# A Perceiver block on one core: keys first, vectors worked out three batches behind their loads, the last output product in another round

## Chip, core and metric

The kernel runs on one core of a Trainium2 chip. The metric is the device time of one execution in microseconds (us). The time before is the median of three runs.

The core has five engines that run side by side, each working through its own instructions in order: TensorE (PE; its weight loads are shown apart as PEld) multiplies matrices, VectorE (DVE), ScalarE (ACT) and GpSimd (POOL) work on vectors, and SyncE (SP) issues the DMAs here. [...] On-chip data lie in SBUF; matmul results lie in PSUM.

## What is computed

Cut to what matters:

```python
x   = x + ln(softmax(q k^T) v @ w_out)      # cross attention: q from layernorm(x), k and v from
                                            # the context (512 rows) and from the latents (64 rows)
x   = x + Wo(rms(softmax(..) - lambda * softmax(..)) @ v)   # differential self attention with rotary q, k
x   = x + down(fp4(silu(gate(fp4(x))) * up(fp4(x))))        # feed-forward, weights fp4 too
```

There are 16 batches, each of 64 latents by 512 (eight tiles of 128 rows, two batches to a tile) and a context of 512 by 512. Cross attention has 8 heads of 64. Self attention takes lambda from four vectors of 32 values (`lambda_q1` and so on), and it scales and shifts its normed output by `ln_w` and `ln_b`, 64 values each. The feed-forward has 1408 hidden columns; its inputs and weights are rounded block by block to fp4.

## The kernel before

Matrices are split into a high and a low half (a rounded copy, and the difference), and each product is the sum of three: high by high, high by low, low by high. `Common.product` (L109) issues them one after the other: for 512 rows of contraction these are 12 matmuls. The high half is usually a ScalarE cast, the low half a subtraction on VectorE or GpSimd in turn.

**Latents** (L427). Tiles 0 and 1 of x are loaded and normed first; `turn` (L478) transposes a tile on TensorE, scales and shifts it with ScalarE (L489) and makes its halves on VectorE (L491, L492). Then, for four groups of two tiles, `heads` (L553) projects q and k (four products of 12 matmuls each), and `values` (L582) projects v (two products). Results go to DRAM scratch and are read back by the batches later. `during(n, ...)` (L541) hangs other work behind the n-th product: splitting weights, the context's weights, the first contexts. In group 0 q comes first, and its evictions lag by two products, because they add `cw.bq`, which `bias` (L494) and `bias_sum` (L505) work out. All weight pieces pass through nine buffers of the tag `raw`.

**Cross attention** (L670). The loop over 16 batches (L927) is an order written out by hand: `keys` and `values` (TensorE, four products each), `scores`, `softmax`, the transposes `turn` and `turn_both`, `finish` for the batch before, and pieces of the next context (`cx.high`, `cx.low`, `cx.stats`, `cx.fetch`). Ten times in a batch it calls `quant.tick()`, which moves the feed-forward's weights along: 35 pieces, a new one every fourth tick, each of ten steps (L260, L163) over all three vector engines and SP. In odd batches from 3 on a finished tile p passes through `out_turn`, `out_product` and `out_norm`, and one batch later through `out_moments`. In batch 2 `att.sa.load()` (L396) loads the vectors of self attention and at once works out lambda. `load_o` and `weight_o` bring `w_out` in batch 0.

**From cross to self attention** (L1021 to L1040) the last tile's output, the splitting of self attention's weights and tile 0 of self attention are interleaved by hand. Then `rest` (L1285) takes a tile n a round: products Wq, Wk and Wv, `rope` (rotations: VectorE, and a last sum on GpSimd, L1122), `end` (L1264: transposes, scores, softmax and sums of tile n, weighing of tile n-1), while tiles n-1 and n-2 are mixed, scaled, turned and projected out.

Up to the end of `rest`, `in_order` (L82) pins each engine's instructions to the order of the program; past it a planner orders the feed-forward by itself. Products share three PSUM buffers of the tag `mm` (transposes too), two pairs of the tag `sim`, and one of the tag `av`.

## Time and profile before

| what | us |
|---|---|
| median of 3 runs (lowest, highest) | 960.89 (959.71, 962.38) |
| the profiled execution | 962.64 |
| its span, first to last instruction | 960.9 |
| its mean granted TensorE clock | 0.984 |

The stages, by windows of the trace: busy us of TensorE, VectorE, ScalarE and GpSimd, and the clock granted to TensorE.

| stage | from, to | PE | DVE | ACT | POOL | clock |
|---|---|---|---|---|---|---|
| first loads and norms | 0, 12 | 2.51 | 5.14 | 6.25 | 4.60 | 1.00 |
| latents, group 0 up to the values | 12, 38 | 24.01 | 16.18 | 11.28 | 8.93 | 0.87 |
| latents, groups 1 to 3 | 38, 88 | 50.00 | 25.58 | 29.22 | 20.59 | 1.00 |
| batch 0 | 93.3, 124.2 | 27.41 | 14.81 | 11.67 | 9.49 | 1.00 |
| batches 1 and 2 | 124.2, 183.3 | 58.03 | 47.09 | 29.88 | 22.85 | 1.00 |
| batch 3, to its output product | 183.3, 214.3 | 26.89 | 21.22 | 11.45 | 9.85 | 0.89 |
| one pair of batches later on | 276.9, 338.1 | 61.19 | 48.64 | 28.68 | 25.86 | 1.00 |
| cross to self attention | 595.6, 634.5 | 32.93 | 23.18 | 13.21 | 20.88 | 0.91 |
| self attention, rounds 3 to 7 | 650, 740 | 83.04 | 70.33 | 31.27 | 42.08 | 1.00 |
| feed-forward | 740, 961 | 208.84 | 169.10 | 57.01 | 26.77 | 0.98 |

How to read it: where TensorE's busy time falls short of a stage's length, it waited; where the clock is under 1.00, its matmuls in part of that stage ran slower than elsewhere. A row of the timeline gives start, length, engine and line, what is written and read, the count, and in brackets the idle time of the engine before it with what ended that. Idle time of another engine costs only if TensorE comes to wait for it.

### The profile page before, as it was taken

The numbers are of one execution on the slowest core, as the hardware profiler recorded it, in microseconds if no ns is written. First come the engines' busy times: TensorE is split into PE (matmuls) and PEld (weight loads), VectorE is DVE, ScalarE is ACT, GpSimd is POOL, SyncE is SP. The second block draws the span as 40 slices with busy tenths as digits, with TensorE's granted clock in tenths as the row PEclk, the third lists the DMA queues.
The fourth block names the chain that finished last, engine by engine and source line by source line (L and its number), as shares of the span: only waits on it lengthen the run. The fifth ranks groups of instructions, "written<-read, shape, count | busy, mean of one in ns | idle before, by whom it ended". The sixth has DMA issues, their size and how long they took to land.

```text
span 960.9 us, 17488 instructions
## 1 busy us (share of the span) xinstructions
PE 911.9 (95%) x6773; PEld 751.3 (78%) x6773; DVE 684.4 (71%) x1396; ACT 383.7 (40%) x738; POOL 332.3 (35%) x362
## 2 busy tenths in 40 slices
PE   5999899999999999999999999889997899999998
PEld 4998677778877878778787888678776688888886
DVE  6434577677788777887787733757878677888875
ACT  4464254443444444444444335333333222222221
POOL 4155253235435353252542504543544320100000
PEclk9999999989999999999999999989999899999999
DMA  6564655544545445454553242400008230000000
GB/s 218 177 230 143 177 183 163 141 136 137 176 140 161 145 144 160 124 161 140 181 171 111 71 124 67 181 18 2 1 1 336 92 121 1 23 12 12 12 12 22
DMA packets 80546, 111.12 MB, mean 116 GB/s; under 512 B 33472, under 2 KB 39120, under 8 KB 79184
## 3 DMA queue, kind: packets, MB, share of 16 engines
q1 hardware_dynamic: 80304, 109.48, 35.4%
q8 instruction: 53, 0.87, 0.4%
q0 software_dynamic: 160, 0.52, 0.2%
q14 instruction: 29, 0.24, 0.1%
HBM read 84.26 MB, written 25.72 MB: 114 GB/s over the span
## 4 chain that ended last, share of the span: by engine, by line
PE 70%; DVE 14%; ACT 5%; issue 4%; DMA 3%; POOL 2%; SPq 1%; ACTq 0%; DVEq 0%; POOLq 0%
PE pk L116 14%; PE pv L116 14%; PE gu L116 10%; PE dn L116 6%; PE av L845 3%; PE sim L777 3%; PE po L116 3%; PE lk L116 2%; PE lq L116 2%; PE lv L116 2%; PE prt L154 2%; PE Wv L116 1%; DVE x L351 1%; DMA dT<-d_d 1%; PE Wq L116 1%
## 5 line engine op out<-in xcount | busy, mean ns | idle before, releaser
L116 PE MATMUL pk<-x,xkh 128*128 128x512 f32 x512 | 132.0, 400 | 2.1 <-DVE k L751 2.1
L116 PE MATMUL pv<-xvh,x 128*128 128x512 f32 x512 | 133.4, 392 | 0.6 <-ACT prT L812 0.6
L116 PEld LDWEIGHTS pk<-x,xkh 128*128 128x128 f32 x512 | 94.8, 190 | 28.0 <-issue 4.4
L116 PEld LDWEIGHTS pv<-xvh,x 128*128 128x128 f32 x512 | 95.2, 188 | 24.2 <-ACT prT L812 4.1
L751 DVE TENSOR_TENSOR k<-pk,row 128x512 f32<-128x512 f32 x64 | 43.9, 686 | 51.9 <-PE pk L116 51.5
L116 PE MATMUL gu<-gT,fx 128*128 128x512 f32 (+1 forms) x288 | 68.7, 387 | 2.8 <-ACT fx L123 2.8
L116 PE MATMUL pk<-x,xkl 128*128 128x512 f32 x256 | 69.4, 393 | 0.0
L116 PE MATMUL gu<-uT,fx 128*128 128x512 f32 (+1 forms) x288 | 68.8, 384 | 0.0
L116 PE MATMUL pv<-xvl,x 128*128 128x512 f32 x256 | 68.5, 389 | 0.0
L800 ACT ACTIVATE pr<-pr,least 128x576 f32<-128x576 f32 x64 | 49.2, 772 | 42.1 <-DVE least L796 41.0
L351 POOL TENSOR_TENSOR x<-raw,x 128x512 fp32r<-128x512 f32 x32 | 44.8, 1401 | 60.3 <-ACT x L345 60.3
L764 ACT ACTIVATE v<-pv,rs 128x512 f32<-128x512 f32 x64 | 43.7, 685 | 53.1 <-PE pv L116 53.0
L116 PEld LDWEIGHTS gu<-gT,fx 128*128 128x128 f32 x288 | 54.3, 194 | 11.5 <-ACT fx L123 3.1
L116 PEld LDWEIGHTS gu<-uT,fx 128*128 128x128 f32 x288 | 52.9, 192 | 7.5
L116 PEld LDWEIGHTS pk<-x,xkl 128*128 128x128 f32 x256 | 48.6, 190 | 10.5
L116 PEld LDWEIGHTS pv<-xvl,x 128*128 128x128 f32 x256 | 48.0, 188 | 10.2
L796 DVE CUSTOM_DVE_ANT_0 pr<-sim,mask 128x576 f32<-128x576 f32 x64 | 45.5, 748 | 7.4 <-PE sim L777 6.9
L116 PE MATMUL dn<-dT,hh 128*128 128x512 f32 x176 | 44.9, 394 | 0.6 <-ACT hh L123 0.6
L304 DVE BATCH_NORM_STATS2 cst<-nat 128x6 f32<-128x512 f32 x64 | 42.9, 670 | 0.0
L845 PEld LDWEIGHTS av<-v,prT 128*64 128x64 f32 x1024 | 36.8, 138 | 5.9 <-issue 5.9
L845 PE MATMUL av<-v,prT 128*64 128x64 f32 x1024 | 41.1, 224 | 0.0
L777 PE MATMUL sim<-k,mask 64*64 64x288 f32 x512 | 39.5, 415 | 0.4 <-DMA mask<-q_d 0.4
(298 smaller groups left out, 1952.6 us busy)
## 6 DMA issues: line engine op xcount, KB each, us to landing
nat<-in_ctx_dram SPq DMA_DIRECT2D x16, 1024.0 KB
raw<-in_ctxT_dram SPq DMA_DIRECT2D x64, 256.0 KB
d_d<-qhl_d SPq DMA_DIRECT2D x11, 512.0 KB
row<-rs_d SPq DMA_DIRECT2D x16, 256.0 KB
g_d<-qhl_g SPq DMA_DIRECT2D x8, 512.0 KB
u_d<-qhl_u SPq DMA_DIRECT2D x8, 512.0 KB
gT<-g_d SPq DMA_DIRECT2D x4, 1024.0 KB
uT<-u_d SPq DMA_DIRECT2D x4, 1024.0 KB
```

Source lines behind the costliest of these rows:

```text
L116: self.nc.tensor.matmul(ps, lhsT=p[i], rhs=p[j], start=start and n == 0, stop=stop and n == last)
L154: self.nc.tensor.transpose(pt[:, c * P : (c + 1) * P], src[:, c * P : (c + 1) * P], self.ident)
L304: nc.vector.bn_stats(st, self.nat[b][:, j, :])
L351: by.tensor_tensor(lo, self.raw[:, c, :], f32(hi), ALU.subtract)
L751: nc.vector.tensor_tensor(k[:, S : S + N], ps, cx.row[b], ALU.mult)
L764: nc.scalar.mul(v, ps, cx.rs[b][:, t : t + 1])
L777: nc.tensor.matmul(pss[r][c * S : (c + 1) * S, h, :half], lhsT=queries[b % 2][rows, m, :], rhs=st["k"][m][rows, at : at + half], start=Tru ...
L796: nc.vector.tensor_tensor_reduce(two(pr), ps[:, :, :half], two(mask), -1.0, BIG, ALU.add, ALU.min, least)
L800: nc.scalar.activation(pr, pr, AF.Exp, bias=least, scale=-1.0, accum_out=st["tot"][:, t : t + 1])
L845: nc.tensor.matmul(st["av"][rows, 2 * a + r, :], lhsT=w[:, rows], rhs=v[:, at : at + S], start=(n == 0), stop=(n == len(pairs) - 1),)
```

## The change

It has seven parts.

1. *Latents.* k's weights are loaded and split ahead of q's, and each group projects k before q. In group 0 the first three k products run their two high-weight sums first (`terms`, `late`), and the low-weight sums follow. Tile 1 is scaled and shifted by VectorE and not by ScalarE, and the halves are made in a call of their own, `halves`. The bias sums of q come behind k's products.
2. *Vectors of self attention.* `sa.load()` in batch 2 only issues the six DMAs of cos, sin and lambda's vectors; `sa.work()` in batch 5 does the arithmetic. `ln_w` and `ln_b` are loaded as rows at the start, transposed by TensorE behind the 17th product, and scaled out of PSUM.
3. *Quantiser.* In batch 0 seven of the ten ticks are left out.
4. *out_turn.* The four ScalarE casts are issued first, then the four VectorE subtractions.
5. *out_norm* is cut in two: the three GpSimd operations are now `out_add`.
6. *Cross to self attention.* Rotations follow their products directly, `sum(0)` is moved past `split("Wo", 0, 1)`, tile 1's products move into this part, the last `out_product` comes behind tile 1's products, `out_norm` behind `end(1)`.
7. *rest* starts at n = 2; there the last tile's `out_add` and `out_moments` come after `out(0)`.

```diff
+    def terms(self, ps, parts, ks, start=True, stop=True):
         terms = [(0, 2), (0, 3), (1, 2)]
...
                 n += 1
+            yield
...
-        lv = cm.const.tile([P, 4, HEAD_DIM], F32, tag="lv", name="lv")
+        self.lv = cm.const.tile([P, 4, HEAD_DIM], F32, tag="lv", name="lv")
         for n, name in enumerate(("lq1", "lq2", "lk1", "lk2")):
-            nc.sync.dma_start(lv[:, n, :], i[name].partition_broadcast(P))
+            nc.sync.dma_start(self.lv[:, n, :], i[name].partition_broadcast(P))
+
+    def work(self):
+        cm, nc, lv = self.cm, self.cm.nc, self.lv
         nc.vector.tensor_tensor(lv[:, :2, :], lv[:, :2, :], lv[:, 2:, :], ALU.mult)
...
-        with nc.allow_non_contiguous_dma(reason="a vector onto partitions"):
-            for n, name in enumerate(("ln_w", "ln_b")):
-                for h in range(2):
-                    nc.sync.dma_start(
-                        self.lnwb[h * S : (h + 1) * S, n : n + 1],
-                        i[name].rearrange("(p o) -> p o", o=1),
-                    )
-        nc.vector.tensor_scalar_mul(self.lnwb, self.lnwb, 1.0 - LAMBDA_INIT)
+    def load_norm(self, pool):
+        self.rows = pool.tile([2, P], F32, tag="lnwb", name="lnwb_rows")
+        for n, name in enumerate(("ln_w", "ln_b")):
+            for h in range(2):
+                self.cm.nc.sync.dma_start(
+                    self.rows[n : n + 1, h * S : (h + 1) * S],
+                    self.i[name].rearrange("(o p) -> o p", o=1),
+                )
+
+    def turn_norm(self):
+        cm, nc = self.cm, self.cm.nc
+        pt = cm.ps_av.tile([P, D], F32, tag="av", name="lnwb_t")[:, :2]
+        nc.tensor.transpose(pt, self.rows, cm.ident[:2, :2])
+        nc.vector.tensor_scalar(self.lnwb, pt, 1.0 - LAMBDA_INIT, None, ALU.mult)
...
-            nc.scalar.activation(ln[:, k, :], src, AF.Identity, bias=bias, scale=scale)
+            if p == 1:
+                nc.vector.tensor_scalar(ln[:, k, :], src, scale, bias, ALU.mult, ALU.add)
+            else:
+                nc.scalar.activation(ln[:, k, :], src, AF.Identity, bias=bias, scale=scale)
+        rows[p] = ln
+
+    def halves(p):
+        g, n = divmod(p, GT)
+        ln = rows.pop(p)
...
-        lag = 2 if (g, what) == (0, "q") else 0
+        late = 3 if (g, what) == (0, "k") else 0
...
+            made.append((m, ps, terms))
+            if m < late:
+                next(terms)
+                next(terms)
+            if m < late - 1:
+                continue
+            for at, done, steps in made:
+                for _ in steps:
+                    pass
+                then()
+                take(at, done)
+            made = []
...
+    weight("k", *range(KC))
     weight("q", *range(KC))
-    weight("k", *range(KC))
...
-    split("q", w_q, 0)
+    high("k", w_k, 0)
     turn(0)
-    split("q", w_q, 1)
     turn(1)
-    split("q", w_q, 2, 3)
+    halves(0)
+    for k in range(1, KC):
+        high("k", w_k, k)
+    halves(1)
     for k in range(KC):
-        high("k", w_k, k)
+        low("k", w_k, k)
     for k in range(KC):
-        bias("q", k)
+        high("q", w_q, k)
+    for k in range(KC):
+        low("q", w_q, k)
...
+    sa.load_norm(pool)
     cx.load(0)
-    during(1, bias_sum, "q", cw.bq, S**-0.5)
     for k in range(KC):
-        during(k // 2, low, "k", w_k, k)
+        during(0, bias, "q", k)
+    during(3, bias_sum, "q", cw.bq, S**-0.5)
+    during(16, sa.turn_norm)
...
+        heads(g, "k", w_k, sc.k, 1.0)
         heads(g, "q", w_q, sc.q, S**-0.5, cw.bq)
-        heads(g, "k", w_k, sc.k, 1.0)
...
             nc.scalar.activation(oh[:, k, :], src, AF.Identity, bias=bias)
+        for k in range(KC):
+            src, bias = pt[:, k * P : (k + 1) * P], cw.bv[:, k : k + 1]
             nc.vector.scalar_tensor_tensor(
...
+        state["oz", p] = z
+
+    def out_add(p):
+        z = state.pop(("oz", p))
         nc.gpsimd.tensor_tensor(z, z, rows_o["g_o"], ALU.mult)
...
+        def tick():
+            if b:
+                quant.tick()
...
-        quant.tick()
+        tick()
...
             out_norm(done)
+            out_add(done)
...
+        if b == 5:
+            att.sa.work()
...
-    out_moments(NT - 2)
     att.product(0, "Wq")
     att.split("Wv", 0, 1)
     finish(B - 1)
+    att.rope(0, "Wq")
     att.split("Wv", 2, 3)
     att.norm(1)
     att.product(0, "Wk")
+    att.rope(0, "Wk")
     out_turn(NT - 1)
-    att.rope(0, "Wq")
     att.product(0, "Wv")
-    att.rope(0, "Wk")
+    att.values(0)
+    out_moments(NT - 2)
+    att.end(0, sum=False)
+    att.split("Wo", 0, 1)
+    att.sum(0)
+    att.product(1, "Wq")
+    att.mix(0)
+    att.product(1, "Wk")
+    att.rope(1, "Wq")
+    att.product(1, "Wv")
+    att.values(1)
+    att.rope(1, "Wk")
+    att.norm(2)
     out_product(NT - 1)
-    att.values(0)
-    att.split("Wo", 0, 1)
+    att.split("Wo", 2, 3)
+    att.end(1)
     out_norm(NT - 1)
-    att.end(0)
-    att.split("Wo", 2, 3)
-    out_moments(NT - 1)
     assert not quant.active and not quant.jobs
+    return {2: lambda: out_add(NT - 1), 3: lambda: out_moments(NT - 1)}
...
-        for n in range(1, NT):
+        for n in range(2, NT):
...
             if n == 2:
+                last[2]()
+                last[3]()
                 ff.weights(("g", 0), ("u", 0))
             self.end(n)
```

More of the change, by code (lines that the diff above doesn't have):

```diff
@@ L107, in two, with product @@
         return self.ps_sim.tile([P, 2, D], F32, tag="sim", name=name)
-    def product(self, ps, parts, ks, start=True, stop=True):
+    def product(self, *args, **kwargs):
+        for _ in self.terms(*args, **kwargs):
+            pass
+    def terms(self, ps, parts, ks, start=True, stop=True):
         terms = [(0, 2), (0, 3), (1, 2)]
@@ L409, in load, with latents, _latents @@
         nc.vector.tensor_scalar(self.neglam, self.neglam, -LAMBDA_INIT, None, ALU.add)
-        with nc.allow_non_contiguous_dma(reason="a vector onto partitions"):
-            for n, name in enumerate(("ln_w", "ln_b")):
-                for h in range(2):
-                    nc.sync.dma_start(
-                        self.lnwb[h * S : (h + 1) * S, n : n + 1],
-                        i[name].rearrange("(p o) -> p o", o=1),
-                    )
-        nc.vector.tensor_scalar_mul(self.lnwb, self.lnwb, 1.0 - LAMBDA_INIT)
-def latents(tc, cm, sc, i, cw, cx):
+    def load_norm(self, pool):
[11 more added lines that the diff above has]
+        nc.vector.tensor_scalar(self.lnwb, pt, 1.0 - LAMBDA_INIT, None, ALU.mult)
+def latents(tc, cm, sc, i, cw, cx, sa):
     with ExitStack() as ctx:
-        _latents(ctx, tc, cm, sc, i, cw, cx)
-def _latents(ctx, tc, cm, sc, i, cw, cx):
+        _latents(ctx, tc, cm, sc, i, cw, cx, sa)
+def _latents(ctx, tc, cm, sc, i, cw, cx, sa):
     nc = tc.nc
@@ L438, in _latents @@
     source = {"q": i["w_q"], "k": i["w_kv"][:, :D], "v": i["w_kv"][:, D:]}
-    raws, lns, zs, mvs, sums = {}, {}, {}, {}, {}
+    raws, lns, rows, zs, mvs, sums = {}, {}, {}, {}, {}, {}
     def load(*tiles):
@@ L570, in heads @@
             ps = cm.mm(f"l{what}_{g}_{m}")[:, : GT * P]
-            cm.product(
-                ps, lambda k: (w[0][:, k, cols], w[1][:, k, cols], hi[:, k, :], lo[:, k, :]), range(KC)
-            )
-            made.append((m, ps))
-            then()
-            if m >= lag:
-                take(*made.pop(0))
-        while made:
-            take(*made.pop(0))
+            terms = cm.terms(
+                ps,
+                lambda k, cols=cols: (w[0][:, k, cols], w[1][:, k, cols], hi[:, k, :], lo[:, k, :]),
+                range(KC),
+            )
+            made.append((m, ps, terms))
[6 more added lines that the diff above has]
+                for _ in steps:
+                    pass
+                then()
+                take(at, done)
+            made = []
         nc.sync.dma_start(dst[g], st)
@@ L665, in _latents @@
                 turn(p)
+                halves(p)
         values(g)
@@ L878, in out_turn @@
             nc.scalar.activation(oh[:, k, :], src, AF.Identity, bias=bias)
+        for k in range(KC):
+            src, bias = pt[:, k * P : (k + 1) * P], cw.bv[:, k : k + 1]
             nc.vector.scalar_tensor_tensor(
@@ L940, in cross_attention @@
         cx.high(b + 1, 1)
-        quant.tick()
+        tick()
         if b:
@@ L951, in cross_attention @@
         cx.high(b + 1, 2)
-        quant.tick()
+        tick()
         if last:
@@ L956, in cross_attention @@
             finish(b - 1)
-        quant.tick()
+        tick()
         if last:
@@ L966, in cross_attention @@
         cx.high(b + 1, 3)
-        quant.tick()
+        tick()
         values(b, 0)
@@ L971, in cross_attention @@
         cx.stats(b + 2, 0)
-        quant.tick()
+        tick()
         if last:
@@ L982, in cross_attention @@
         cx.stats(b + 2, 1)
-        quant.tick()
+        tick()
         if b == 0:
@@ L1262, in out, with end @@
         self.nc.vector.tensor_tensor(cm.x[t], ps, cm.x[t], ALU.add)
-    def end(self, n):
+    def end(self, n, sum=True):
         if n < NT:
@@ L1281, in end, with rest @@
             self.rms(n - 1)
-        if n < NT:
+        if n < NT and sum:
             self.sum(n)
-    def rest(self, ff):
+    def rest(self, ff, last):
         norms = iter([step for t in range(2) for step in ff.norm_steps(t)])
@@ L1293, in step @@
             next(steps, lambda: None)()
-        for n in range(1, NT):
+        for n in range(2, NT):
             self.product(n, "Wq")
-            if 0 <= n - 2:
-                self.scale(n - 2)
+            self.scale(n - 2)
             self.product(n, "Wk")
             self.mix(n - 1)
-            if 0 <= n - 2:
-                self.turn_o(n - 2)
+            self.turn_o(n - 2)
             self.rope(n, "Wq")
@@ L1310, in rest @@
                 step(norms)
-            if 0 <= n - 2:
-                self.out(n - 2)
+            self.out(n - 2)
             if n >= 4:
@@ L1506 @@
     quant = Quantise(cm, sc, i)
-    latents(tc, cm, sc, i, cw, cx)
+    latents(tc, cm, sc, i, cw, cx, sa)
     w2 = ctx.enter_context(tc.tile_pool(name="work_2", bufs=1, reuse_waits="tile"))
@@ L1511 @@
     att = SelfAttention(cm, i, sa, w1, w2)
-    cross_attention(tc, cm, sc, i, cw, cx, w1, w2, att, quant)
-    att.rest(ff)
+    last = cross_attention(tc, cm, sc, i, cw, cx, w1, w2, att, quant)
+    att.rest(ff, last)
     ff.rest()
```

## The prediction

> **What bounds the kernel.** I read the page's busy shares first, then who waited for whom, asked of TensorE, then the timeline where those waits lie.

> ```profile
> span 960.9 us, 17488 instructions
> ...
> PE 911.9 (95%) x6773; PEld 751.3 (78%) x6773; DVE 684.4 (71%) x1396; ACT 383.7 (40%) x738; POOL 332.3 (35%) x362
> ...
> PE   5999899999999999999999999889997899999998
> ...
> PEclk9999999989999999999999999989999899999999
> ```

> TensorE is busy in 911.9 of 960.9 us, so only 49 us of idle time, and matmuls run at a lowered clock, can be won: no operation of TensorE leaves the program. The lower digits sit at the start, in slices 8 to 9 (168 to 216 us), and from slice 26 on.

> ```profile
> PE ot L154 <- DVE on L1234: 7.4, 4, 3.3
> ...
> PE qt L154 <- POOL rc_q L1122: 4.0, 1, 4.0
> PE po L116 <- ACT v L764: 3.2, 3, 1.1
> ...
> PE bq L509 <- DVE ws_bq L501: 2.0, 1, 2.0
> PE pk L116 <- DVE k L751: 2.1, 1, 2.1
> ...
> PE ot L154 <- DVE k L751: 2.0, 1, 2.0
> ```

> Columns: total us, times, longest. The diff touches the qt, bq and pk waits and the second ot; between 196 and 580 us TensorE has 380.2 busy of 384.

> **Part 1, the vectors' load at b = 2.**

> ```profile
> 187.97 0.23 DVE L404 TENSOR_TENSOR lv<-lv 128x64 f32<-128x64 f32 x1 [5.91 <-DMA lv<-in_lk_dram]
> 192.04 0.66 PE L154 MATMUL ot<-ident,o 128*128 128x128 f32 x4 [2.04 <-DVE k L751]
> 194.76 3.78 PE L116 MATMUL pk<-x,xkh 128*128 128x512 f32 x8 [2.07 <-DVE k L751]
> ```

> VectorE stands 5.91 us at L404 before a load that was just issued; behind it are queued the context's statistics, the quantiser and two key evictions (L751), which hold PSUM buffers, so TensorE stops twice and then runs slowly: eight matmuls in 3.78 us, against 1.98 for the same form at 186.02. From keys(3,0) at 183.30 to the output product at 214.35 is 31.05 us; the same stretch two batches on, 251.56 to 276.91, is 25.35. The whole stall is 5.7 us. Afterwards six DMAs are still issued there (2.75 us of the SP queue by the rows at 182.01 to 184.81; the lnwb four, 2.4 us, go to the start), but nothing waits for them until b = 5. There the arithmetic costs VectorE 0.23 + 0.22 + 0.16 + 0.15 and a trip through ScalarE, shown as 0.27 idle: about 1.1 us. Behind it are queued statistics, and in batch 5 VectorE idles 1.4 us or more before a key eviction (row at 254.48), so I take 0.3 lost: **-5.4**, between -6 and -4. The four lnwb row loads, one transpose and one PSUM read in the latents' second group cost under 0.3 us, beside 60 us in which TensorE never waits.

> **Part 2, the start.** Before, q's projection stops at 17.08 for the bias sums (2.0 idle), runs the sums (1.5), and restarts at half pace until 26. With k first the sums have 48 matmuls of cover. If rows held at their lone durations: first matmul at 12.1 (transpose done 9.0; four scalings on VectorE at 0.3 us, estimated from L879's 0.35 on the same 128x128 out of PSUM; halves 0.43 + 0.69 + 0.43), k's 48 matmuls by 19.4 (18 at 0.21 us, as at 11.98, the rest at 0.12), sums 1.0, q 5.8, transposes 0.9: values begin at 27.1 instead of 32.5, -5.4. But:

> ```profile
> 7.73 0.68 DVE L455 TENSOR_TENSOR wql<-raw_q,wqh 128x512 fp32r<-128x512 f32 x1
> ...
> 12.57 1.78 DVE L455 TENSOR_TENSOR wql<-raw_q,wqh 128x512 fp32r<-128x512 f32 x1
> ```

> The same instruction takes 0.68 alone and 1.78 beside a GpSimd subtraction. [...] This speaks against the change: GpSimd now has four low halves (k1, k3, q1, q3) ready from 9.9 us on, while VectorE is kept at the scalings until 10.4 and only then makes the latents' halves. Taken in turns, GpSimd holding some 1.15 us each time (the 1.78 less 0.68 gives 1.1), the halves end at 11.6, 13.4, 14.9 and 16.7, the bias at 22.4; the first matmul is at 15.0, values at 30.7. [...] I take **-1.8**; between +1 (one turn more) and -5.4.

> **Part 3, no quantiser at most of batch 0.**

> ```profile
> 110.15 0.69 DVE L177 TENSOR_REDUCE qm_g<-qw_g 128x32 f32<-128x512 f32 x1 [6.11 <-DMA qw_g<-in_w_gate_dram]
> ...
> 121.17 1.20 PE L116 MATMUL pv<-xvh,x 128*128 128x512 f32 x4 [0.57 <-ACT prT L812]
> ```

> VectorE waits 6.11 us for a weight piece, queued late behind key loads on SP; the softmax stands behind it, and TensorE idles 0.93 and 1.54 us at the transposes. Both go. But the last wait stays and grows: values(0,3) needs a PSUM buffer that the prT copy frees, and that copy is behind woh's casts, which wait for raw_wo, issued at 113.78 by an SP queue that is full from 94 on. Two removed issues bring it forward 1.2 us, and 256 KB fewer in flight about 0.9 (at 270 GB/s): **-2.2** instead of the 3.1 of idle; between -5 (batch 1's later wait of 1.07 goes too) and -0.5. Since seven ticks vanish, every later quantiser step falls on another place of its batch. The 1.0 to 1.1 us wait before the output product in four of six pairs of batches (62.6 against 61.2 us) comes from a cast (L271) ahead of v's eviction; in odd batches that cast now comes a slot earlier, but a ScalarE step that waits for VectorE (L188) takes its slot. I take **-1**: between -4.4 (four waits gone) and +3.

> Splitting out_turn's loops takes away the 0.42 us turns of ScalarE and VectorE (27.4 us of VectorE idle over eight calls), but TensorE waits there only 0.5 us, in the last call, so it is counted in part 4 alone.

> **Part 4, from cross to self attention.**

> ```profile
> 626.36 0.66 PE L154 MATMUL qt<-ident,rc_q 128*128 128x128 f32 x4 [4.05 <-POOL rc_q L1122]
> 627.76 1.12 PE L154 MATMUL kt<-ident,rc_k 128*128 128x128 f32 x4 [0.75 <-POOL rc_k L1122]
> ```

> From Wq of tile 0 (595.59) to Wq of tile 2 (634.46) is 38.9 us. The chain of waits runs out_turn, product, moments, zl, softmax, sums, out_moments on VectorE; only then come tile 1's rotations, and after 4.05 us idle the next matmuls run slowly (wt 1.97, later 1.15). Worked through again in the new order with the rows' durations: tile 0's rotations follow their products directly [...], qt 608.5, scores 610.3, Wq of tile 1 611.1 (was 613.85), softmax ends 614.3, sum and mix 619.6, tile 1's rotations on GpSimd 622.4 and 623.8; meanwhile TensorE has tile 1's products and the moved output product until 622.2. Then qt, kt, wt, zt, scores, weighing: Wq of tile 2 at 628.2, **-6.3**. Given back: out_norm's 0.8 on VectorE comes between the sums and scale, where

> ```profile
> 655.64 0.68 DVE L1234 TENSOR_TENSOR on<-o,rstd_o 128x512 f32<-128x512 f32 x1
> ...
> 656.38 0.65 PE L154 MATMUL ot<-ident,on 128*128 128x128 f32 x4
> ```

> shows no slack: ot starts as scale's result lands. With the tighter start of that round 1.4 us. And in round 2 three GpSimd products (L896 to L898, 1.3 each = 3.9) run before out_moments, where VectorE waits in order, with the next zl, softmax, sums and scale behind it: zl moves about 1.9, so +1.9 at the next ot. Part 4: **-3.0**, between -7.5 and -0.5. From round 3 on the order is the old one.

> **Sum.** -5.4 - 1.8 - 2.2 - 1 - 3.0 = -13.4. The profiled execution took 962.64 us (span 960.9 plus 1.74 around it): 949.2. It lay 1.75 above the median 960.89, so the forecast is **947.5**. The feed-forward's order beyond the fixed part is chosen by a planner and may shift by 1.5 either way.

> **Rivals.** (a) *Everything hidden is won*: VectorE and GpSimd don't take turns at the start (-5.4), the four waits vanish (-4.4), out_add's wait hides (part 4 -5): with -5.4 and -3 that is -23, about 938. For it: most stalls are single events; against: 1.78 beside 0.68. (b) *The transition and the start are given back*: GpSimd's pieces delay the first matmul, the waits at ot repeat (0 and -0.5), leaving parts 1 and 3: -5.9 - 2.2 = -8, about 953. For it: the zero slack at ot. (c) *The quantiser's new place* makes a new ScalarE wait before v's eviction, in every batch from 2 to 14. It has to eat 13.4 plus 2.9 us over 13 batches, 1.25 us each, to end slower; at 1.5 us it gives 967. For it: the present wait is 1.1 us in four odd batches. Against: even batches show none, and 384-wide pieces lost it with 0.15 us less on each row. (d) *No effect*: the removed stalls are all refilled; against it, the b = 2 stall has no work beside it.

> **Chances.** Forecast, within some 5 us: 66%; (a) 16%; (b) 12%; (c) 3%; (d) 3%. A measurement here tells about 0.3% (2.9 us) from nothing: faster 94%, same 3%, slower 3%. Range 938 to 955: it takes in (a) and (b).

> **What would show it.** Right: no VectorE idle of several us in b = 2; first lk matmul near 15 and values near 31; no L177 in batch 0 before the first softmax, and a wait of some 1.5 us at values(0,3); qt of tile 1 without 4 us of idle; a wait of 1 to 2 us at ot of tiles 0 and 1. Wrong: the first lk matmul near 12 (turns not taken) or beyond 16; waits "po <- ACT v" in most batches (c); Wq of tile 2 less than 3 us nearer to Wq of tile 0.

## The result, and the profile after

The changed kernel takes 943.75 us (943.18 to 944.45), the kernel before 960.30 (958.79 to 962.38) in the same series: ratio 0.9826, 95% interval 0.9805 to 0.9848, or 16.55 us less. In a later series it took 945.93 beside 961.20 (ratio 0.9841, 0.9828 to 0.9855), at a mean granted clock of 0.991 to 0.993 instead of 0.994 to 0.996. The forecast was 947.5, with a range of 938 to 955.

The page of the changed kernel, its first lines and the slices (span 960.9 before):

```profile
span 941.4 us, 17506 instructions
...
PE 902.7 (96%) x6774; PEld 744.8 (79%) x6774; DVE 689.1 (73%) x1400; ACT 381.9 (41%) x734; POOL 324.9 (35%) x362
...
PE   4999999999999999999999999999998799999998
...
PEclk9999999999999999999999999999999899999999
```

TensorE has one matmul more (the transposed norm rows). Of the 19.5 us between the two spans 10.3 are idle time of TensorE (49.0 before, 38.7 after) and 9.2 are busy time (911.9 before, 902.7 after). The second part is pace: the clock records of the two traces show 30.7 us at half clock before and 10.2 after, and half of that difference is 10.2. So the stops that went had cost twice, 10.3 us as idle time and 9.2 us as slow work. The lower digits of TensorE in slices 5, 26 and 27, and of the clock in slices 9 and 27, are gone. Whom TensorE waited for (total us, times, longest):

```profile
PE ot L160 <- DVE on L1300: 10.2, 6, 3.5
PE lk L121 <- DVE lnh L516: 5.7, 1, 5.7
...
PE pv L121 <- ACT prT L854: 2.3, 1, 2.3
```

The waits of before at qt (4.0 us), at bq (2.0), at pk and the second ot (2.1 and 2.0), and the three at po (3.2) are no longer in the view. The one at pv, in batch 0, has grown (0.6 before), and so have that of the first product at the start (3.0 at lq before, 5.7 at lk now, because the halves come later) and those at ot (7.4 before). Cut into stages at TensorE's first rows of each product, the two traces give (us):

| stage | before | after | difference | forecast |
|---|---|---|---|---|
| start to the first values | 32.52 | 30.65 | -1.87 | -1.8 |
| values to the first keys | 60.83 | 61.16 | +0.33 | under +0.3 |
| batch 0 | 30.68 | 31.15 | +0.47 | -2.2 |
| batch 1 | 30.29 | 28.99 | -1.30 | in batch 0's |
| batch 2 | 28.98 | 28.98 | 0 | 0 |
| batch 3 to its output product | 30.98 | 24.07 | -6.91 | -5.4 |
| on to batch 15's output product | 371.51 | 367.79 | -3.72 | -1 |
| on to Wq of tile 0 | 9.80 | 9.81 | +0.01 | 0 |
| Wq of tile 0 to Wq of tile 2 | 38.87 | 31.61 | -7.26 | -6.3 |
| Wq of tile 2 to tile 4 | 32.58 | 35.37 | +2.79 | +3.3 |
| Wq of tile 4 to the end | 289.10 | 287.14 | -1.96 | 0 |

The sum is -19.4, the spans' difference but for 0.1 us; the end here is the start of the last row of matmuls. The last row of the table is no effect of the change. Between its first gate product and that end the feed-forward took 214.37 us before and 212.71 after; in the second trace of the same changed kernel it took 215.45, and in eleven other kernels of this study, none of which touches it, 213.89 to 215.65. The windows of its first 20 us (length, busy us of PE, PEld, DVE, ACT and POOL, granted clock, DMA share, GB/s), first trace, then second:

```profile
724.00:744.00 20.00, 18.31 (x131) 15.03 (x132) 14.41 (x29) 5.56 (x8) 7.18 (x12) 0.91 0.48 168
```

```profile
723.00:743.00 20.00, 18.32 (x119) 14.84 (x120) 12.84 (x24) 5.56 (x8) 5.25 (x5) 0.77 0.48 168
```

One program, two executions, and a clock of 0.91 or 0.77 in the same 20 us. In all fourteen traces the feed-forward's length, less TensorE's idle time in it (6.4 to 8.0 us) and half of its time at half clock (6.8 to 13.0 us), is 202.5 to 203.0 us: the spread is made by these two alone. So times are compared below by their ratios, and single effects by the stage in which they lie.

### The profile page after: what moved, and what is told of

Read it like the earlier page. It is cut to its first block, busy times and chain, and to the rows that moved or that the text cites. A ratio compares the mean times of both kernels' runs of the same rounds, so it can differ in the third digit from the quotient of the medians.

```text
span 941.4 us, 17506 instructions
## 1 busy us (share of the span) xinstructions
PE 902.7 (96%) x6774; PEld 744.8 (79%) x6774; DVE 689.1 (73%) x1400; ACT 381.9 (41%) x734; POOL 324.9 (35%) x362
## 4 chain that ended last, share of the span: by engine, by line
PE 79%; DVE 11%; POOL 4%; ACT 3%; DMA 2%; issue 1%; SPq 1%; ACTq 0%; DVEq 0%; POOLq 0%
PE pv L121 18%; PE pk L121 18%; PE gu L121 10%; PE dn L121 6%; PE av L887 4%; PE sim L819 4%; PE prt L160 3%; PE lk L121 3%; PE lq L121 2%; PE lv L121 2%; PE po L121 2%; DVE ex L1228 1%; DVE mx L1227 1%; POOL rc_q L1188 1%; PE ht L160 1%
## 5 line engine op out<-in xcount | busy, mean ns | idle before, releaser
L121 PEld LDWEIGHTS pk<-x,xkh 128*128 128x128 f32 x512 | 93.7, 188 | 25.4 <-issue 3.9
L121 PE MATMUL gu<-gT,fx 128*128 128x512 f32 (+1 forms) x288 | 66.8, 379 | 2.8 <-ACT fx L129 2.8
L121 PEld LDWEIGHTS pv<-xvl,x 128*128 128x128 f32 x256 | 48.6, 190 | 10.4
L121 PEld LDWEIGHTS pk<-x,xkl 128*128 128x128 f32 x256 | 48.1, 188 | 10.3
L854 ACT COPY prT<-prt 128x512 f32<-128x512 f32 x64 | 34.1, 585 | 18.1 <-PE prt L160 18.1
```

The costliest lines, as they stand in the source:

```text
L121: self.nc.tensor.matmul(ps, lhsT=p[i], rhs=p[j], start=start and n == 0, stop=stop and n == last)
L854: nc.scalar.copy(prT, pt.rearrange("p (j q) -> p j q", q=P))
```

## The experiments

Kernels of one series ran on one chip, beside the kernel before. Times are medians.

### One stop at a time

**The vectors alone.** The kernel before, with the arithmetic at b = 5 and all else as it was:

```diff
         if b == 2:
             att.sa.load()
+        if b == 5:
+            att.sa.work()
```

> The kernel before with the vectors' arithmetic (and only it) moved from their loads at b = 2 to b = 5; the four norm rows are still loaded at b = 2, one element to a partition. The stall as costed in the prediction: VectorE's 5.91 us idle at b = 2 goes, TensorE's two waits of 2.0 and 2.1 us and the slow matmuls after them too; from the first key product of batch 3 to the output product of tile 0 the stretch falls from 31.05 to 25.4 us, and the time by 5.4 us, to about 955.4 where before is 960.84. Rival: the wait only moves to b = 5, where the norm rows' own landing or the trip through ScalarE stops VectorE in the same way: the stretch of batch 6 grows by 3 us or more, and 2 us at most are won.

956.89 beside 961.33: ratio 0.9950 (0.9935 to 0.9965), -4.4 us. Batch 3's stretch is 26.03, that is -4.95 where some 5.6 were expected: ahead of its output product TensorE now stands 1.04 us for v's eviction, a wait that the stall had covered. From batch 5's output product to batch 7's, where the arithmetic now falls, it takes 61.66, against 61.23 before: 0.4 lost, not 3. In the changed kernel the late arithmetic reads, on VectorE:

```profile
273.71 0.22 DVE L413 TENSOR_TENSOR lv<-lv 128x64 f32<-128x64 f32 x1
273.96 0.22 DVE L415 TENSOR_REDUCE dots<-lv 128x2 f32<-128x64 f32 x1
274.45 0.72 DVE L417 TENSOR_TENSOR neglam<-dots 128x1 f32<-128x1 f32 x1 [0.27 <-ACT dots L416]
```

No idle time before L413 (5.91 us before), and 0.27 for the trip through ScalarE.

**The loops of out_turn alone.** The kernel before, with one line added:

```diff
             nc.scalar.activation(oh[:, k, :], src, AF.Identity, bias=bias)
+        for k in range(KC):
+            src, bias = pt[:, k * P : (k + 1) * P], cw.bv[:, k : k + 1]
             nc.vector.scalar_tensor_tensor(
```

> The kernel before with only the loop in out_turn split in two (ScalarE's four reads of the transposed outputs first, then VectorE's four). The prediction gave this nothing in the batches. If the four waits of 1.05 us before the output product need both the quantiser's old place and the turns that ScalarE and VectorE take in out_turn (0.42 us idle each): they fall to about 0.2 us, from the output product of batch 3's round to the last one in the batches it is 369.4 instead of 371.4, and the time is 2 to 3.5 us less (with batch 3's own wait, and 0.4 before the last tile's product), about 958. If the prediction was right that the loops are worth nothing in the batches: the four waits stay at 1.05 us and the time stays within 0.5 us.

957.54 beside 961.33: ratio 0.9959 (0.9946 to 0.9973), -3.8 us for a reordering of eight instructions. From batch 3's output product to batch 15's it is 368.84 instead of 371.51, and batch 3's stretch is 0.6 shorter. The forecast had given this nothing in the batches. VectorE, ScalarE and TensorE in batch 5 before, then the same three with the loops split:

```profile
262.38 0.35 DVE L879 SCALAR_TENSOR_TENSOR ol<-ot,bv,oh 128x128 fp32r<-128x128 f32 x1 [2.25 <-ACT oh L878]
263.17 0.35 DVE L879 SCALAR_TENSOR_TENSOR ol<-ot,bv,oh 128x128 fp32r<-128x128 f32 x1 [0.43 <-ACT oh L878]
...
265.01 0.68 DVE L751 TENSOR_TENSOR k<-pk,row 128x512 f32<-128x512 f32 x1
...
274.88 0.69 DVE L270 STREAM_TRANSPOSE qhl_u<-qw_u 128x512 f32<-128x512 f32 x1
...
275.65 0.62 ACT L271 CAST qhl_u<-qhl_u 128x512 fp32r<-128x512 f32 x1 [2.88 <-issue]
276.18 0.68 ACT L764 ACTIVATE v<-pv,rs 128x512 f32<-128x512 f32 x1
...
276.91 1.20 PE L116 MATMUL po<-woh,oh 128*128 128x512 f32 x4 [1.05 <-ACT v L764]
```

```profile
263.64 1.13 DVE L881 SCALAR_TENSOR_TENSOR ol<-ot,bv,oh 128x128 fp32r<-128x128 f32 x4 [3.02 <-ACT oh L878]
264.69 0.68 DVE L751 TENSOR_TENSOR k<-pk,row 128x512 f32<-128x512 f32 x1
...
274.56 0.69 DVE L270 STREAM_TRANSPOSE qhl_u<-qw_u 128x512 f32<-128x512 f32 x1
...
275.34 0.62 ACT L271 CAST qhl_u<-qhl_u 128x512 fp32r<-128x512 f32 x1 [2.89 <-issue]
275.86 0.68 ACT L764 ACTIVATE v<-pv,rs 128x512 f32<-128x512 f32 x1
...
276.60 1.19 PE L116 MATMUL po<-woh,oh 128*128 128x512 f32 x4 [0.25 <-ACT v L764]
```

The instruction ahead of these on VectorE, L270 at 259.44 before, runs 0.48 later with the loops split, and the key eviction behind them (L751) 0.32 earlier: 0.80 gained. From that eviction to the transposition L270 (274.88 before, 274.56 with the loops split) VectorE shows no idle time in either trace, so the 0.80 arrives there whole. ScalarE's cast of its result (L271) stands ahead of v's eviction, and TensorE's wait falls from 1.05 to 0.25: the same 0.80, some twenty VectorE instructions and twelve microseconds further on.

**The quantiser's place**, from both sides: the changed kernel with the old place, and the kernel before with the new one.

```diff
-        self.clock, self.active = 0, []
+        self.clock, self.active = 3, []      # in the changed kernel
+        self.clock, self.active = 1, []      # in the kernel before
```

> The changed kernel with the quantiser's counter started at 3 instead of 0, so that from batch 1 on every step of the quantiser falls on the same place of its batch as before the change, while batch 0 stays free of it. If the four waits of some 1.05 us before the output product (TensorE for v's eviction on ScalarE) are made by the place of the quantiser's steps alone: the four come back, the stretch from the first key product of batch 1 to the last output product of the batches is 4 to 5 us longer, and the time rises by 4 to 5 us to about 948.5. If instead the relief of batch 0 or the vectors' move took those waits away: none comes back and the time stays within 1 us of 943.7.

> The kernel before with the quantiser's counter started at 1 instead of 0, nothing else: the steps fall where the changed kernel has them, batch 0 keeps its quantiser. Place alone: the four waits of 1.05 us vanish, 4 to 5 us less than before, about 956 where before is 960.3; in batch 0 VectorE's wait for the weight piece may move by one step, within 1 us. If the place is worth what the prediction took, it is 1 us less; if a new ScalarE wait comes in its place (the prediction's third rival), it is slower.

The first took 947.19 beside 960.84 (ratio 0.9853, 0.9831 to 0.9874); its four executions spread over 5.5 us, and by the ratios it is 0.1 to 0.3% longer than the changed kernel, within the intervals. By stages: batch 3 is 24.54 (24.07), and on to batch 15's product 369.45 (367.79), so 2.1 us, not 4 to 5; the waits come back as 0.2 us. The second took 961.91 beside 960.84 (ratio 1.0004, 0.9996 to 1.0013): nothing. It wins 1.86 us on the way to batch 15, and loses 2.07 in batch 3, where VectorE's idle time before the vectors' load is 7.55 us instead of 5.91:

```profile
189.45 0.22 DVE L404 TENSOR_TENSOR lv<-lv 128x64 f32<-128x64 f32 x1 [7.55 <-DMA lv<-in_lk_dram]
```

In the rest of its trace batch 0 is 1.62 shorter and batch 1 2.14 longer than before. Together with the loops, in the stretch from batch 3's to batch 15's output product (us):

| | old place | new place |
|---|---|---|
| loops joined | 371.51 | 369.65 |
| loops split | 368.84 (alone), 369.45 (with the other edits) | 367.79 |

The two figures of the changed kernel (369.45 and 367.79) contain the arithmetic of the vectors, too, 0.4 us in the run with the vectors alone. Either edit alone takes most of the 1.05 us waits (0.25 with the loops, 0.08 to 0.25 with the place); of the stretch the loops take the larger part.

**The output weight's loads ahead of batch 0**, in the changed kernel:

```diff
     around(1, 0, 1)
+    load_o(0)
+    load_o(1)
     for b in range(B):
...
-        if b == 0:
-            load_o(0)
-            load_o(1)
         values(b, 1)
```

> The changed kernel with the loads of the output weight's first two row blocks issued ahead of batch 0 instead of in its middle. If TensorE's 2.31 us before the fourth value product of batch 0 comes from woh's casts waiting for those loads, and the slow matmuls after it (1.89 us for four, 1.07 elsewhere) from that wait: both go, batch 0 from its first key product to that of batch 1 falls from 31.15 to about 27.2, and the time falls by about 4 us to 939.7. If the slow matmuls have another cause: 2.3 us less, and the row of 1.9 us stays. If the load only takes the place of another one on the same queue (the keys' ends or the queries of batch 0): the wait reappears at the scores of batch 0 and the time falls by less than 1 us.

941.62 beside 960.84: ratio 0.9795 (0.9779 to 0.9811). Batch 0 is 27.21; TensorE no longer waits at pv, the matmuls there keep their pace (1.98 us for eight), and at the scores it waits 0.85 us for the queries (0.6 in the changed kernel), so the wait did not move there. ScalarE and TensorE of the changed kernel, first trace, then TensorE of its second:

```profile
116.50 0.62 ACT L129 CAST woh<-raw_wo 128x512 fp32r<-128x512 f32 x1 [4.48 <-DMA raw_wo<-in_w_out_dram]
...
117.89 1.07 ACT L854 COPY prT<-prt 128x512 f32<-128x512 f32 x2
```

```profile
118.52 1.89 PE L121 MATMUL pv<-xvh,x 128*128 128x512 f32 x4 [2.31 <-ACT prT L854]
120.21 1.91 PE L121 MATMUL pv<-xvl,x 128*128 128x512 f32 x4
121.91 1.21 PE L121 MATMUL pv<-xvh,x 128*128 128x512 f32 x4
```

```profile
118.08 1.20 PE L121 MATMUL pv<-xvh,x 128*128 128x512 f32 x4 [2.24 <-ACT prT L854]
119.12 1.08 PE L121 MATMUL pv<-xvl,x 128*128 128x512 f32 x4
```

The cast waits 4.48 us for raw_wo, the prT copy stands behind it, the values behind the copy, as forecast. After 2.31 us the matmuls run at nearly half their pace for some 3.4 us (the three rows begin 3.39 us apart, first to last, against 1.96), which costs about 1.5 more; after 2.24 us in the second execution they don't (its third row begins at 120.04). In six traces with this batch 0 (both of the changed kernel, and the runs on the place, the start, the moments and the product) the wait is 1.6 to 2.5 us and batch 0 takes 28.97 to 31.25: three with slow matmuls (all 31.15 or more), three without (29.58 or less). Batch 1 evens some of it out: it takes 29.0 after a slow batch 0 and 30.2 to 30.5 after a quick one, with a wait of 1.0 to 1.1 us at the latents' part of the weighing (prl). Batches 0 and 1 together: 61.64 is the mean of three traces with the old batch 0 (before, vectors alone, loops alone; 60.96 to 62.25), 59.89 that of the six (59.20 to 60.31), and 56.85 it is with the loads ahead. The gain is thus about 3 us, in the stretch where it was expected.

**The start: low halves on VectorE**, in the changed kernel:

```diff
-        by = (nc.vector, nc.gpsimd)[k % 2]
+        by = nc.vector if name in early else (nc.vector, nc.gpsimd)[k % 2]   # early: k and q of the latents
```

> The changed kernel with the low halves of the keys' and the queries' weights all made on VectorE, none on GpSimd. If the latents' halves at the start (1.08, 1.48, 1.64 and 1.64 us) are slowed by taking turns with GpSimd's subtractions: they fall to 0.43 and 0.69, the first key product of the latents starts at about 11.5 instead of 14.74, and the values at about 28 (VectorE has four more pieces of 0.69 us to do), 2 to 3 us less in all, about 941.3. If the halves are slow for another reason: their rows stay above 1 us, the four pieces come on top of them, and the start is 1 to 3 us longer.

VectorE and GpSimd in the changed kernel, then VectorE in this one, where GpSimd has none of these subtractions:

```profile
10.44 1.08 DVE L516 CAST lnh<-ln 128x512 fp32r<-128x512 f32 x1
11.55 1.64 DVE L517 TENSOR_TENSOR lnl<-ln,lnh 128x512 fp32r<-128x512 f32 x1
13.11 1.48 DVE L516 CAST lnh<-ln 128x512 fp32r<-128x512 f32 x1
...
9.97 2.67 POOL L472 TENSOR_TENSOR wkl<-raw_k,wkh 128x512 fp32r<-128x512 f32 x2 [2.50 <-ACT wkh L468]
12.60 3.12 POOL L472 TENSOR_TENSOR wql<-raw_q,wqh 128x512 fp32r<-128x512 f32 x2
```

```profile
10.35 0.42 DVE L517 CAST lnh<-ln 128x512 fp32r<-128x512 f32 x1
10.80 0.69 DVE L518 TENSOR_TENSOR lnl<-ln,lnh 128x512 fp32r<-128x512 f32 x1
11.41 0.42 DVE L517 CAST lnh<-ln 128x512 fp32r<-128x512 f32 x1
```

Without GpSimd's subtractions the same instructions take 0.42 and 0.69, the first k product starts at 11.98 instead of 14.74 and the values at 27.79 instead of 30.65. So the subtractions beside them made these rows long; that the two engines take turns was the author's reading, and the rows don't show in what way one holds up the other. In the time, 943.46 beside 960.84 (ratio 0.9816, 0.9802 to 0.9830), the 2.86 us don't appear against the changed kernel's 0.9826 (against its 0.9841 of the later series 2.4 us do): in this trace the feed-forward took 215.65 us, with 13.0 us at half clock against 6.8 in the changed kernel's first trace. Whether that was chance was left to the runs together, below.

### From cross to self attention

**The last output product back in its old round**, in the changed kernel:

```diff
     att.product(0, "Wv")
+    out_product(NT - 1)
     att.values(0)
...
     att.norm(2)
-    out_product(NT - 1)
```

> The changed kernel with the last tile's output product put back into the first round of self attention (after tile 0's Wv product, as before), its norm and what follows left where the change has them. If the product is worth its own length as cover for tile 1's rotations: TensorE stands up to 3.2 us before tile 1's query transposes again, and from the Wq product of tile 0 to that of tile 2 it is about 34.8 us (31.61 with the change, 38.87 before), about 946.5 in all. If the earlier rotations and moments did it alone: the stretch stays within 0.5 us of 31.6 and TensorE waits nowhere longer.

948.48 beside 961.33: ratio 0.9865 (0.9850 to 0.9879), some 3 us longer than the changed kernel. From Wq of tile 0 to Wq of tile 2 it is 36.55, 4.94 more than with the change, where 3.2 were expected. TensorE in this kernel, then its first row of the four in the changed one, which has no wait:

```profile
610.92 1.12 PE L160 MATMUL qt<-ident,rc_q 128*128 128x128 f32 x4 [2.79 <-POOL rc_q L1188]
612.35 1.11 PE L160 MATMUL kt<-ident,rc_k 128*128 128x128 f32 x4 [0.31 <-POOL rc_k L1188]
613.39 1.97 PE L1264 MATMUL wt<-ident,w 64*64 64x64 f32 x32
615.29 1.11 PE L160 MATMUL zt<-ident,z 128*128 128x128 f32 x4
```

```profile
608.68 0.60 PE L160 MATMUL qt<-ident,rc_q 128*128 128x128 f32 x4
```

2.79 us are the missing cover. The rest is pace: from qt to the next Wq this kernel takes 7.57 us, the changed one 5.53 for the same operations (wt 1.15, zt 0.66), and the granted clock is 0.53 here:

```profile
610.00:614.00 4.00, 2.77 (x20) 2.04 (x22) 2.84 (x5) 1.03 (x2) 3.96 (x3) 0.53 0.00 0
```

Of the change's -7.26 in this stretch the product's move is 4.94 by these two traces. The remaining 2.3 are the split loops and the other moves, which shorten the wait at qt from 4.05 to 2.79; these weren't tried apart. In the run with only the loops split the stretch is 36.49, 2.4 less than before, but only 0.8 of it lies ahead of tile 0's query transposes, where the loops act; the wait at tile 1's (qt) is 4.05 as before, and from there on it takes 6.53 us instead of 8.10 because the slow matmuls ended sooner.

**The last moments a round later**, in the changed kernel:

```diff
             if n == 2:
                 last[2]()
-                last[3]()
                 ff.weights(("g", 0), ("u", 0))
+            if n == 3:
+                last[3]()
```

> The changed kernel with the last tile's moments one more round later, ahead of round 3's end instead of round 2's; GpSimd's three products stay in round 2. If the 1.71 us that TensorE waits at tile 1's output transposes comes from VectorE standing at these moments for GpSimd's products: it goes, the stretch between the Wq products of tiles 3 and 4 falls from 18.16 to about 16.5, and the next ones stay at 16.5. [...] If it moves along with the moments: the next stretch grows by as much. In the time it is 1.7 us at most, about 942, no more than the spread of a few runs.

943.52 beside 961.33: ratio 0.9812 (0.9799 to 0.9824). VectorE in the changed kernel, then TensorE there, then TensorE in this one:

```profile
631.16 0.69 DVE L145 BATCH_NORM_STATS2 st_a<-x 128x6 f32<-128x512 f32 x1 [3.54 <-POOL x L946]
631.89 0.18 DVE L146 BATCH_NORM_AGGREGATE x_mv<-st_a 128x2 f32<-128x6 f32 x1
631.99 0.66 DVE L130 TENSOR_TENSOR zl<-zt,zh 128x512 fp32r<-128x512 f32 x1
```

```profile
638.90 0.66 PE L160 MATMUL ot<-ident,on 128*128 128x128 f32 x4 [1.71 <-DVE on L1300]
```

```profile
635.78 0.66 PE L160 MATMUL ot<-ident,on 128*128 128x128 f32 x4
```

VectorE stands 3.54 us for GpSimd's last product with zl and the softmax behind it. Without that the stretch from tile 3 to tile 4 falls from 18.16 to 16.49. The next one took 16.86 here, 16.50 in the changed kernel; but the same 16.9 came in two runs without this edit (both of the place), and 16.5 in two runs with it below, so it doesn't belong to the edit: some 1.7 us are won in the stretch. In the time they don't stand out (0.9812 beside 0.9826).

### Once more, and together

**The changed kernel unaltered**, in the series of the combinations:

> The changed kernel once more, unaltered, for a base in the same series and to see what moves between two executions of one program. Batch 0, from its first key product to that of batch 1, took 31.15 us in the changed kernel's first trace and 28.97 and 29.10 in two others with the same batch 0; the feed-forward, from its first gate product to the end, between 212.7 and 215.7 us with the same order of work. If matmuls at a lowered clock come by chance after a wait of 1.6 us or more: both stretches lie anywhere in these ranges again, the start and the batches from 2 on within 0.3 us of the first trace, and the time is 942 to 945.

945.93, above the range that was expected, with a start of 30.22 (0.43 from the first trace, where 0.3 was allowed), batches 0 and 1 of 29.58 and 30.28, the stages from batch 2 to the feed-forward within 0.3 of the first trace, and the feed-forward at 215.45: the chance lies in batch 0 and in the feed-forward, as expected, and to a smaller part in the start.

**Loads ahead and moments later**, then **the start as well**, then **the last norm behind tile 0's scaling** on top:

> The changed kernel with two edits together: the output weight's first loads ahead of batch 0, and the last tile's moments a round later. If their gains add: batch 0 near 27.2 us, the Wq stretch of tiles 3 to 4 near 16.5, 3 to 5 us less than the changed kernel of the same series, about 939.5. If the one gives back the other's: as the changed kernel within 1 us.

> The same two edits and the low halves of the keys' and queries' weights on VectorE. By the traces of the start alone (values 2.86 us earlier): 2.9 us less than with the two edits, about 936.7, 6 to 8 less than the changed kernel. If what the start wins is given back in the feed-forward by a lower granted clock (as in the run with that edit alone, whose feed-forward took 2.9 us longer): the same time as with the two edits, with the feed-forward at 215 us or more again. If that was chance: the feed-forward lies anywhere between 212.7 and 215.7.

> The three edits, and the last tile's output norm behind the scaling of tile 0 in round 2 instead of ahead of it. If VectorE's 0.8 us of norm between the sums and the scaling makes TensorE's 0.77 us wait at tile 0's output transposes: it goes, the Wq stretch of tiles 2 to 3 falls from 17.2 to about 16.4, and the time by 0.8 against the three edits. If the PSUM buffer that the product then holds longer stops the next product instead: a wait of 0.5 us or more at Wk or Wv of that round, and nothing is won.

| kernel | median | ratio (interval) | start | batch 0 | tiles 2 to 3 | 3 to 4 | feed-forward |
|---|---|---|---|---|---|---|---|
| changed | 945.93 | 0.9841 (0.9828 to 0.9855) | 30.22 | 29.58 | 17.22 | 18.15 | 215.45 |
| two edits | 940.54 | 0.9787 (0.9774 to 0.9800) | 31.21 | 27.03 | 17.22 | 16.49 | 214.33 |
| three edits | 938.19 | 0.9760 (0.9745 to 0.9775) | 27.93 | 27.06 | 17.21 | 16.49 | 213.89 |
| with the norm | 940.39 | 0.9780 (0.9762 to 0.9798) | 27.90 | 27.40 | 17.20 | 16.51 | 214.34 |

The gains add. Two edits win 5.4 us on the changed kernel (about 3 and 1.7 by their stretches alone; the changed kernel's feed-forward was long in this series), the start 2.35 more, and here the feed-forward is short: what the start wins isn't given back there. The run with the start alone showed less in its time, and its executions ran at a lower clock: their mean granted clock was 0.990 to 0.994, against 0.994 to 0.996 for the changed kernel in its first series and 0.995 for the three edits. By estimate, 0.003 less of some 940 us is 3 us, about what is missing. That isn't the edit's doing, as far as these runs show: the unaltered changed kernel had 0.991 to 0.993 in this series. Three edits make the best kernel, 7.7 us below the changed one and 23.0 below the kernel before. The norm's place wins nothing: tile 0's wait at ot (0.81 in the three edits) goes, but the stretch stays at 17.20, with 0.27 at kt for GpSimd's rotation, which VectorE now feeds 0.8 later. The work was moved on the same chain, not off it.

## Why the prediction held, and where it was wrong

The forecast was 3.75 us too high (1.6 against the later series). Its -13.4 between two traces stands against -19.4, of which 2.0 is chance in the feed-forward. The other 4.0 are errors of both signs: the stretches from batch 3 to batch 15 won 4.2 more than forecast, part 4 1.5 more, batches 0 and 1 1.4 less. That they partly cancel is luck.

- **The vectors, -5.4**: right in mechanism, a little large. It was -5.7 for the stall less 0.3. Alone they give -4.95 in the stretch, with 0.4 lost at b = 5, and -4.4 in the time; the wait of 1.04 behind the stall was not foreseen.
- **The start, -1.8**: GpSimd's subtractions delayed it as forecast, with the first k product at 14.74 (15.0 forecast) and the values at 30.65 (30.7). That -1.87 between the two traces fits so well is in part luck: the values began at 30.86 to 32.52 in four traces with the old start and at 30.22 to 31.42 in seven with the new one, 1.3 apart in the mean. The figure reckons with rows stretched beside GpSimd (1.78 against 0.68) and not with lone ones, and the run without GpSimd's halves bears this out: they cost 2.86 us. The turns of some 1.15 us were an estimate from that pair of rows. Projecting k first was not tried without the rest.
- **Batch 0, -2.2**: too much for the profiled execution, -0.83 with batch 1, and near for the mean of the traces (61.64 less 59.89 is 1.75). The chain was right (raw_wo, woh, prT, values). Its 270 GB/s was an estimate; the trace of before shows 255 from 113.78 to 121.00 us. Leaving out the seven ticks was not tried alone; VectorE's wait for a weight piece did not go with them, but is now 8.98 us long at 125.35, in batch 1, where TensorE in the first trace doesn't come to wait for it. The wait was 1.6 to 2.5 us where 1.5 was taken, and three of six traces pay another 1.5 or so in slow matmuls, a price that the sum had counted for the stalls of parts 1 and 4 but not for the wait left here.
- **The quantiser's place, -1, and out_turn's loops**: the step that failed. The prediction said of the loops that "TensorE waits there only 0.5 us, in the last call, so it is counted in part 4 alone". It looked at who waited at out_turn itself. But VectorE has no idle time from there to the transposition that v's eviction waits behind, so 0.80 us lost in turns came out as TensorE's wait at the output product. The loops alone give -2.7 from batch 3 on and -0.6 in batch 3; the place gives 2.1 in the changed kernel, and nothing in the kernel before. The waits that it spoke of come in three of the six pairs of batches (62.63 us each against 61.15 to 61.24), not in four; the fourth is the one of 1.04 behind the stall of batch 3. With the 4.95 of the vectors taken off, these stretches fell by 5.7 us, not by 1.
- **Part 4, -3.0**: -4.47. The given-back waits were right in place and nearly in size (+1.11 and +1.68 for +1.4 and +1.9); the run with later moments shows the cause of the second. For the first, the norm, the run that moved it took the wait away and won nothing, so that its part in the +1.11 isn't shown. The gain was 7.26 for 6.3: the product's cover was there, but the slow matmuls behind the wait, up to 2 us of them, were not fully in it.
- **Rivals**: the quantiser's place didn't bring a new wait in every batch; the old one went. "Everything hidden is won" was right for the waits at po, wrong for the start and for out_add's wait, which came (1.71 at ot). "Given back" was right that GpSimd's pieces delay the first matmul and that the waits at ot come, wrong that they eat the transition's gain.
- **Readings**: TensorE's own digits are 9 in slices 8 and 9; there only the clock's digit of slice 9 is lower. Between the start and slice 26 its only lower digit is that of slice 5, in batch 0. The output product of batch 3 begins at 214.28, so its stretch was 30.98.

## What to carry to other kernels

When an instruction is sped up, follow its engine forward to the next idle time, not only to its own readers: on a VectorE without gaps, 0.8 us lost in hand-overs to ScalarE came out as a wait of TensorE twelve microseconds later, and issuing all of one engine's part before the other's won 3.8 us. Waits of TensorE of 2.31 and 2.79 us were followed here by slow matmuls that cost another 1.5 and 2.04 us, one of 2.24 us by none: removing such a wait, or covering it with a product moved there, can be worth more than its length, and leaving one lets the time vary (batch 0 took 28.97 to 31.25 us in six traces). Work moved later helps only if it leaves the chain: while VectorE stood 3.54 us for GpSimd at the last moments, zl and the softmax behind them waited too.

## What the runs showed of the hardware

```profile
115.34:118.76 3.42, 1.11 (x5) 0.62 (x4) 0.97 (x4) 2.02 (x4) 1.56 (x2) 1.00 0.88 232
118.76:122.17 3.41, 3.41 (x9) 2.62 (x9) 0.00 (x0) 2.90 (x7) 1.25 (x2) 0.50 0.63 160
```

```profile
114.35:117.77 3.42, 1.49 (x7) 0.90 (x5) 1.59 (x6) 1.46 (x3) 0.87 (x1) 1.00 1.04 291
117.77:121.18 3.41, 3.10 (x13) 2.55 (x14) 0.00 (x0) 3.22 (x8) 1.64 (x2) 1.00 0.59 157
```

The same program after nearly the same wait was granted 0.50 or 1.00. In the first trace the wait lies within one step, with 2.31 us of it idle; in the second it runs over into the next, with 1.93 idle in the first of the two. The other four fit: steps with 2.32 and 2.06 us idle were followed by a fall, with 1.63 and 1.61 by none. In the traces of before and of the changed kernel (first), from their first clock records at 16.10 and 19.77 us on, each fall came behind a step with 1.65 to 2.91 us idle: 1.65 (before, from 753.38) and 1.67 (changed, from 733.16) were followed by one, 1.68 (before, from 111.67) and 1.73 (changed, from 719.50) were not. What sets the clock, these records don't show.

GpSimd's subtractions stretched VectorE's casts too, which read one tile: by 0.66 and 1.06 us (0.42 to 1.08 and 1.48), its subtractions with two inputs by 0.95 (0.69 to 1.64). Their own rows were 1.27 to 1.71 us long there, against 1.28 for the same form at 22.8 us in that trace.
